# A four-layer graph attention kernel: other step costs for the clock that spaces out row and tile work

## The chip, the core and the metric

The kernel runs on one core of one Trainium2 chip. The metric is the device time of one execution in microseconds (us), the median of the runs shown. Engines are named as in the profile: PE is the matrix engine (TensorE), PEld its loading of weights, DVE the vector engine, ACT the scalar engine, POOL the engine that issues the gathers here (GpSimd), SP the one that issues most plain transfers.

## What is computed

The input is x (4096 nodes by 256 features) and one adjacency matrix adj (4096 by 4096, sparse, denser towards the low node numbers). Four layers of graph attention follow each other, each with a layer norm, a ReLU and a residual. Cut to what matters:

```python
def layer(x, f):                       # the same around all four
    h = relu(layernorm(x))
    return x + f(h)

def f0(h):                             # f1: the same, with elu around it
    g = h @ W.T + b_W
    e = leaky_relu((g @ a1)[:, None] + (g @ a2)[None, :] + b_a, 0.2)
    return softmax(where(adj > 0, e, -big), axis=1) @ g

def f2(h):                             # four heads of 64 columns each
    g = einsum("ni,hio->hno", h, W)
    e = leaky_relu(src[:, :, None] + dst[:, None, :], 0.2)
    return concat_heads(softmax(where(adj > 0, e, -inf)) @ g)

def f3(h):                             # two softmaxes, of e and of -e
    p = softmax(where(adj > 0,  e, -big)) @ h
    q = -softmax(where(adj > 0, -e, -big)) @ h
    return elu(concat(p, q) @ wtrans)
```

## The kernel before, in words

Nodes are cut into 32 tiles of 128 (T = 0 to 31). A target tile's sum over its sources is worked in *steps*. A **dense** unit takes four target tiles at once and goes through all 32 source tiles, one per step (in layer 2 one per step and head). A **listed** unit takes one target tile and goes through the first four source tiles and then through CAPS[T] groups of 128 listed sources, which are gathered by row number from a table in DRAM (L1228, s_gg). How many blocks of four tiles are dense is DENSE = (4, 2, 1, 1) for layers 0 to 3; the rest is listed.

In `run` (L1191) one plan of steps goes through four stages, by LEAD = (0, 2, 3, 6): a step is fetched (its gather is issued), two steps later `begin` (layer 2's share of the weights on ACT, L1018), three steps later `weigh` (the weights on DVE, L1032, L1041), six steps later `multiply` (PE, L1068, in layer 2 L1093). All engines work through their queues in the order in which this plan issues the instructions.

Between the steps other work is strewn in, held in two queues of Python generators, `posts` and `lists_q`:

- what ends a tile: `end1`, `end2`, `end3` (layer 1: ACT and DVE, L1131 to L1135; layer 2: a copy s_o on ACT, L1148, transposes s_oT on PE, L1155, then DVE, L1160 to L1165);
- `node_rows` (L683), which makes the rows of the next layer for two tiles: statistics (L693, L694), Ln and Exp on ACT (L697, L698), z (L702), three small DVE instructions (L709 to L711), transposes s_tp on PE (L716), copies s_hT on ACT (L718), projections s_pj on PE (L748), their scaling on ACT or DVE (L770 to L783) and the store of the rows to the table (L729);
- in layer 0, `list_sources` (L819), which finds the lists of sources from the adjacency matrix, a block of four tiles at a time (DVE L825 to L875, PE idx_ps L900, the list in L910). Once a tile's list exists, its masks are gathered (`gather_masks`, L928), one after each dense step of layer 0; what is then still missing is gathered in one go before that tile's first row gather (L1223).

A generator yields the time for which it wants to be left alone (4.0, 3.0, 1.5, 1.0 or nothing). The delay is measured by a clock that is not the chip's: after each step's multiply the plan adds the step's assumed `cost` to it. Then up to `rates` entries of the queues go on, of the first two in `posts` and the first in `lists_q`, if the clock has passed the time that they wait for. So a delay of d lasts as many steps as their costs take to add up to d. Where a step needs rows which are not made yet, `ensure` (L676) drives the posts on without regard to the clock. After the dense steps with which a layer opens, all rows of the layer must be there before the first gather: layer 1 opens with 16 dense steps, layer 2 with 36, layer 3 with 16 (L1476).

The transposes s_tp, s_sT (L966) and s_oT, the projections s_pj and the lists' idx_ps share a pool of two PSUM buffers (tag "mm", `ps_mm`); the sums of the units share six (`ps_acc`), gathered rows seven or nine in SBUF.

In layer 1 the masks of tiles 8 to 15 come with the gathered rows and are copied away by ACT (L1240); so ACT's queue waits for the gathers there. In layer 2 that holds for tiles 4 to 7.

The cost lines that the change touches are the default of `Unit.__init__` (L985), the listed units of layer 0 (L1378), the dense units of layers 1 and 2 (L1463; layers 0 and 3 take the default) and the listed units of layers 1 to 3 (L1471).

## Time and profile before

| what | us |
|---|---|
| median of 3 runs | 1701.94 (1697.17 to 1703.21) |
| the profiled execution | 1796.08 |
| its span, first to last instruction | 1794.3 |
| layer 0 (in the profiled execution) | about 30 to 517 |
| layer 1 | 517 to 841 |
| layer 2 | 841 to 1366 |
| layer 3 | 1366 to 1783 |

The profiled execution is longer than the runs without a profile, so durations from the trace add up to its own time and not to the median. In the profile's lines, Lnnn is the line of the kernel, `out<-in` names the tiles, x is the number of instructions, and the bracket at the end of a timeline line gives the idle time of the engine before it and what ended it. A matrix multiplication in f32 shows as two records.

### The profile page before, as it was taken

Reading aid. Unit: us, or ns where it says so; the run is one execution under the profiler, and the core shown is the slowest. Engines: PE = TensorE matmul, PEld = TensorE weight load, DVE = VectorE, ACT = ScalarE, POOL = GpSimd, SP = SyncE. Lnnn points to the kernel's source line nnn. Section 1 sums busy time; section 2 is a strip of 40 time slices with the busy share of each in tenths; the row PEclk is TensorE's granted clock in tenths of the full one; section 3 lists DMA queues with packets and bytes.
Section 4 is the critical chain, followed back from the end, with each engine's and each line's share of the span. In section 5 each row is a group of like instructions: output and inputs, shape, how many; then the busy total and the mean of one; then the engine's idle time right before and its main releaser. Section 6 shows DMA issues by size and latency. Waiting matters only on the chain.

```text
span 1794.3 us, 29158 instructions
## 1 busy us (share of the span) xinstructions
PE 1660.2 (93%) x9268; PEld 1384.3 (77%) x9268; DVE 1319.1 (74%) x3908; ACT 631.0 (35%) x1915; POOL 960.5 (54%) x930
## 2 busy tenths in 40 slices
PE   6998899799889999888999999988889999999997
PEld 4886777678778778676577878788888888888876
DVE  6787899777744676556788888877785566777755
ACT  5630010020120232333467666788884011111101
POOL 8836666646535656553353444444561666655453
PEclk9999999999879999989999999999999999999999
DMA  7888778853244444543233332323342665666553
GB/s 258 301 299 281 242 244 251 264 143 110 60 135 138 134 117 134 147 132 106 82 94 86 90 90 81 98 82 83 99 116 75 197 208 175 183 180 178 160 165 107
DMA packets 152237, 274.70 MB, mean 153 GB/s; under 512 B 21423, under 2 KB 75340, under 8 KB 152076
## 3 DMA queue, kind: packets, MB, share of 16 engines
q0 software_dynamic: 45584, 130.39, 26.8%
q1 hardware_dynamic: 105656, 141.83, 24.2%
q8 instruction: 77, 1.26, 0.3%
q14 instruction: 84, 0.69, 0.1%
q10 hardware_dynamic: 836, 0.53, 0.1%
HBM read 231.76 MB, written 40.90 MB: 152 GB/s over the span
## 4 chain that ended last, share of the span: by engine, by line
PE 78%; DVE 8%; issue 4%; DMA 3%; POOL 3%; ACT 2%; another core or an unknown queue 2%; SPq 0%; POOLq 0%; DVEq 0%; ACTq 0%
PE s_acc L1068 44%; PE s_accm L1093 20%; PE s_pj L748 8%; DVE s_p L1032 3%; PE idx_ps L900 2%; PE s_tp L716 2%; PE s_sT L966 2%; DMA s_gg<-table,idx 1%; DMA s_raw<-in_adjT 1%; ACT s_p L1018 1%; DVE s_m L1322 1%; POOL s_z L702 1%; POOL s_gg L1228 1%; DVE s_p L1041 0%
## 5 line engine op out<-in xcount | busy, mean ns | idle before, releaser
L1228 POOL DMA_INDIRECT s_gg<-table,idx x715 | 757.9, 1060 | 733.5 <-PE s_acc L1068 228.6
L1032 DVE SCALAR_TENSOR_TENSOR s_p<-s_grow,s_gg,mlist 128x128 f32<-128x128 f32 x994 | 310.1, 346 | 143.0 <-PE s_acc L1068 85.9
L1068 PE MATMUL s_acc<-s_gg,s_p 128*128 128x257 f32 x1430 | 353.8, 390 | 9.9 <-DVE s_p L1032 7.8
L1068 PEld LDWEIGHTS s_acc<-s_gg,s_p 128*128 128x128 f32 x1430 | 270.5, 194 | 53.6 <-DVE s_p L1032 12.6
L1068 PE MATMUL s_acc<-g,s_p 128*128 128x257 f32 x1152 | 292.5, 397 | 14.2 <-DVE s_p L1032 5.3
L1068 PEld LDWEIGHTS s_acc<-g,s_p 128*128 128x128 f32 x1152 | 220.0, 198 | 49.7 <-issue 12.3
L1032 DVE SCALAR_TENSOR_TENSOR s_p<-s_grow,pre,mpre 128x128 f32<-128x128 f32 (+1 forms) x576 | 189.2, 369 | 49.4 <-PE s_acc L1068 30.5
L1093 PE MATMUL s_accm<-s_p,s_gg 128*65 128x128 f32 x1744 | 204.7, 273 | 1.7 <-issue 1.6
L1068 PE MATMUL s_acc<-s_gs,s_p 128*128 128x257 f32 x896 | 203.6, 380 | 0.0
L1032 DVE SCALAR_TENSOR_TENSOR s_p<-s_grow,s_gs,s_ms 128x512 f32<-128x512 f32 x224 | 161.9, 748 | 50.7 <-PE s_accm L1093 24.7
L748 PE MATMUL s_pj<-s_w,s_hT 128*128 128x259 f32 (+3 forms) x640 | 175.9, 417 | 24.9 <-ACT s_hT L718 9.5
L1093 PEld LDWEIGHTS s_accm<-s_p,s_gg 128*65 128x65 f32 x1744 | 193.2, 138 | 5.3 <-issue 2.8
L1018 ACT ACTIVATE s_p<-s_grow,s_minus,s_gg 128x128 f32<-128x128 f32 x436 | 186.7, 485 | 25.9 <-PE s_accm L1093 15.0
L1068 PE MATMUL s_acc<-pre,s_p 128*128 128x257 f32 x768 | 184.0, 384 | 5.5 <-ACT s_y L1179 3.5
L1068 PEld LDWEIGHTS s_acc<-s_gs,s_p 128*128 128x128 f32 x896 | 169.4, 190 | 24.7 <-issue 0.6
L972 ACT ACTIVATE s_grow<-s_sT 128x256 f32<-128x256 f32 (+2 forms) x136 | 46.8, 367 | 379.3 <-PE s_sT L966 260.9
L748 PEld LDWEIGHTS s_pj<-s_w,s_hT 128*128 128x128 f32 x640 | 126.3, 205 | 56.4 <-ACT s_hT L718 14.2
L1068 PEld LDWEIGHTS s_acc<-pre,s_p 128*128 128x128 f32 x768 | 144.5, 192 | 28.4 <-ACT s_y L1179 3.9
L928 POOL DMA_INDIRECT mlist<-mask_t,idx x105 | 122.1, 1162 | 65.1 <-issue 30.0
L1093 PE MATMUL s_accm<-s_p,pre 128*65 128x128 f32 (+1 forms) x928 | 122.2, 286 | 2.6 <-issue 2.5
L1093 PEld LDWEIGHTS s_accm<-s_p,pre 128*65 128x65 f32 x928 | 105.1, 139 | 21.0 <-issue 18.3
L1018 ACT ACTIVATE s_p<-s_grow,s_minus,pre 128x128 f32<-128x128 f32 x224 | 95.0, 485 | 23.2 <-issue 18.9
(126 smaller groups left out, 1743.5 us busy)
## 6 DMA issues: line engine op xcount, KB each, us to landing
s_raw<-in_adjT SPq DMA_DIRECT2D x128, 512.0 KB
s_gs<-table SPq DMA_DIRECT2D x28, 516.0 KB
s_gg<-table,idx POOLq DMA_INDIRECT x715
mask_t<-s_m SPq DMA_DIRECT2D x35, 256.0 KB
table<-s_g SPq DMA_DIRECT2D x28, 258.0 KB
s_ms<-mask_t SPq DMA_DIRECT2D x28, 256.0 KB
table<-s_m SPq DMA_DIRECT2D x21, 256.0 KB
table<-g SPq DMA_DIRECT2D x8, 516.0 KB
```

The source lines that it names most:

```text
L702: (nc.gpsimd if L.l == 0 else nc.vector).tensor_scalar(z, x[:, T, :], mv[:, k, 0:1], 0.0, op0=ALU.subtract, op1=ALU.max)
L716: nc.tensor.transpose(tp[:, c, :], zs[k][:, c * P : (c + 1) * P], ident)
L748: nc.tensor.matmul(ps, lhsT=hT[:, c, :], rhs=L.w[:, c, k * (D + 6) : k * (D + 6) + cols], start=(c == 0), stop=(c == 1),)
L900: nc.tensor.matmul(ps[:, 0:cap], lhsT=first[:, :, j % half], rhs=val[:, 0:cap, j * IT + t], start=(j == 0), stop=(j == JT - 1),)
L928: nc.gpsimd.indirect_dma_start(out=mlist[:, OFFS[T] + k, :], out_offset=None, in_=mask_t[T // IT], in_offset=bass.IndirectOffsetOnAxis(ap= ...
L966: nc.tensor.transpose(ps[:, h - h0, it, :], L.s[:, T0 + it, h : h + 1].to_broadcast([P, P]), ident)
L972: nc.scalar.activation(grow[:, h1:h2, :], ps[:, h1 - h0 : h2 - h0].rearrange("p h a b -> p h (a b)"), AF.Exp, scale=scale,)
L1018: nc.scalar.activation(w[:, h, :], u.grow[:, h, :], AF.Relu, scale=g[h][:, n - 1 : n], bias=minus)
L1032: nc.vector.scalar_tensor_tensor(p[:, k, :], u.grow[:, h, :], g[k][:, n - 1 : n], m, op0=ALU.min if L.l == 3 and h == 1 else ALU.max, op1= ...
L1068: nc.tensor.matmul(u.accs[it][h], lhsT=p[:, k, it * P : (it + 1) * P], rhs=g[k][:, 0:n], start=first, stop=last,)
L1093: nc.tensor.matmul(u.regions[h], lhsT=g[k][:, 0 : DH + 1], rhs=p[:, k, :],  start=first and (u.nt > 1 or h == 0), stop=last, skip_group_ch ...
L1228: nc.gpsimd.indirect_dma_start(out=wide, out_offset=None, in_=L.table, in_offset=bass.IndirectOffsetOnAxis(ap=index[T][:, k : k + 1], axis=0),
```

## The change

Only costs are exchanged; no instruction is added or taken away.

```diff
-        def __init__(u, L, T0, nt, n, get, big=None, heads=None, like=None, cost=1.7, nact=0, rates=(2, 0, 0), per=1):
+        def __init__(u, L, T0, nt, n, get, big=None, heads=None, like=None, cost=2.1, nact=0, rates=(2, 0, 0), per=1):
...
-            u = Unit(L0, T, 1, DP + CAPS[T], listed_sources(L0, T, gat0), cost=0.45, rates=(1, 2, 0))
+            u = Unit(L0, T, 1, DP + CAPS[T], listed_sources(L0, T, gat0), cost=0.55, rates=(1, 2, 0))
...
-                    cost=0.9 if l == 2 else 1.7,
+                    cost=0.55 if l == 2 else 2.1,
...
-                L, T, 1, DP + CAPS[T], listed_sources(L, T, gat), cost=(0, 0.9, 1.2, 0.9)[l], nact=(0, 0, 2, 0)[l]
+                L, T, 1, DP + CAPS[T], listed_sources(L, T, gat), cost=(0, 0.55, 0.9, 1.05)[l], nact=(0, 0, 2, 0)[l]
```

So a dense step counts 2.1 instead of 1.7 in layers 0, 1 and 3, and 0.55 instead of 0.9 in layer 2 (where a step is one head of one source tile). A listed step counts 0.55 instead of 0.45 in layer 0, 0.55 instead of 0.9 in layer 1, 0.9 instead of 1.2 in layer 2 and 1.05 instead of 0.9 in layer 3.

## The prediction

> **What bounds the kernel now.** I read the page's parts 1 and 2, then stretches cut at the layers' borders, then TensorE's waits in each stretch, then the timeline around the places where rows are spread.

> ```profile
> PE 1660.2 (93%) x9268; PEld 1384.3 (77%) x9268; DVE 1319.1 (74%) x3908; ACT 631.0 (35%) x1915; POOL 960.5 (54%) x930
> ...
> 30.00:517.00 487.00, 445.22 (x2534) 372.59 (x2532) 386.95 (x968) 103.67 (x378) 298.96 (x259) 0.94 0.69 214
> 517.00:841.00 324.00, 290.35 (x1298) 242.07 (x1299) 195.44 (x598) 85.20 (x305) 173.95 (x174) 0.95 0.48 137
> 841.00:1150.00 309.00, 304.22 (x1900) 221.42 (x1899) 270.86 (x794) 196.04 (x527) 132.28 (x121) 0.99 0.31 86
> 1150.00:1352.00 202.00, 180.13 (x1456) 168.95 (x1455) 158.48 (x563) 170.84 (x500) 98.10 (x95) 0.98 0.35 97
> ...
> 1366.00:1783.00 417.00, 411.27 (x1912) 355.39 (x1910) 275.24 (x877) 50.36 (x132) 228.59 (x218) 1.00 0.57 170
> ```

> Part 1, then stretches (length; busy PE, PEld, DVE, ACT, POOL; clock, DMA): layer 0, layer 1, layer 2 with its dense block, layer 2's tiles alone, layer 3. TensorE is busy 1660.2 of 1794.3 us. The 134.1 us of idle lie 41.8 in layer 0, 33.7 in layer 1, 4.8 and 21.9 in layer 2, 5.7 in layer 3, 26.3 before 30 and after 1783. This execution took 1796.08 us, the median is 1701.94: 94 us of it are absent from ordinary runs, and TensorE's busy time would nearly fill them. So less than half of the idle can be real, and no change of order can win much. I apply differences in us to the median unscaled.

> The change moves only work spread by the clock: tile ends, next rows, layer 0's lists. Its places:

> ```profile
> 145.11 0.44 PE L716 MATMUL s_tp<-s_ident,s_z 128*128 128x128 f32 x2 [1.16 <-ACT s_hT L718]
> 146.01 1.14 PE L748 MATMUL s_pj<-s_w,s_hT 128*128 128x259 f32 x4 [0.46 <-ACT s_hT L718]
> ...
> 499.61 1.03 POOL L928 DMA_INDIRECT mlist<-mask_t,idx  x1 [0.31 <-issue]
> 506.51 0.95 POOL L928 DMA_INDIRECT mlist<-mask_t,idx  x1 [0.30 <-issue]
> 507.76 0.94 POOL L1228 DMA_INDIRECT s_gg<-table,idx  x1 [0.30 <-issue]
> ...
> 584.63 1.17 PE L748 MATMUL s_pj<-s_w,s_hT 128*128 128x268 f32 x4 [1.91 <-issue]
> ...
> 867.06 1.97 PE L748 MATMUL s_pj<-s_w,s_hT 128*128 128x268 f32 x8
> 869.71 0.42 DVE L776 TENSOR_TENSOR s_g<-s_pj,s_re 128x256 f32<-128x256 f32 x1 [0.48 <-ACT s_re L774]
> 872.91 0.95 POOL L1228 DMA_INDIRECT s_gg<-table,idx  x1 [42.66 <-PE s_accm L1093]
> 883.09 1.72 PE L1093 MATMUL s_accm<-s_p,s_gg 128*65 128x128 f32 x11
> ...
> 819.30 0.69 PE L716 MATMUL s_tp<-s_ident,s_z 128*128 128x128 f32 x2 [4.70 <-issue]
> ```

> These are timeline lines (start, us, engine, line, work, idle before). They show a transpose held while a list's idx_ps occupies one of two s_mm buffers; a burst of mask gathers ahead of layer 0's last tile; a projection held in layer 1; layer 2's last rows, 4 to 7, projected just before its first gather; a transpose held in layer 1's end, where ACT's copies of masks wait for gathers.

> [...] the transpose at 819.30 held every later matmul of TensorE for 4.70 us. [...] the last row is ready at 869.71 + 0.42 = 870.13 and the gather that reads the table starts 2.8 us later.

> **The change part by part.** A delay d at cost c lasts ceil(d/c) steps. So 1.5 in layer 1's tiles goes from 2 steps to 3 and 4.0 from 5 to 8; in layer 2's dense steps 4.0 goes 5 to 8, 1.5 from 2 to 3; in layer 2's tiles 1.0 goes 1 to 2 and 3.0 from 3 to 4; in layer 0's dense steps a list's 4.0 goes 3 to 2. In layer 3 the row and tile delays of 1.5 stay 1 step (dense) and 2 (tiles). No instruction is added or dropped; each is only placed earlier or later. I counted every placement by pump's rule.

> Real pitch, from groups of matmuls: 16 records of a dense step pair in layer 1 take 614.11 - 610.64 = 3.47 us, so a record 0.217, a dense step (8) 1.74, a tile step (2) 0.43. In layer 2, 20 dense records take 8.75, so a dense step (2) 0.87; a tile step (8) 3.66/4 = about 0.9. The new 0.55 for layer 2's dense steps is thus below the trace.

> *Layer 0's end, a gain.* The first list's index comes 3 steps sooner, and mask gathers, one per dense step, run about 8 steps further ahead. Before, dense steps end with 8 gathers undone: two fall before tile 30's rows (479.74, 480.99), six before tile 31's (499.61 to 507.46). After, five. A gather takes 0.95 plus 0.30: 1.25 us. The two have 6.1 us of POOL idle behind them at 482.4, so they are hidden. The sixth stands straight before the last tile's six row gathers, where TensorE waits: -1.3. Bounds -3.8 (three count) and 0.

> *Layer 0's lists, a loss.* Lists that come 3 to 5 steps sooner meet the next layer's row work at other steps. Transposes placed while an idx_ps is open go from 7 to 13: rows 4 to 11 come in, 14 and 15 go out, 3 pairs net. With one buffer, second transpose and projection queue behind ACT's s_hT: 1.16 + 0.46 here, 0.32 + 0.46 at 131: 1.2 us a pair, 3.6. Dense steps behind have up to 3 weights ready, so part returns later: +2.5. Bounds -2 (the pairs removed at 470 and 482 idled 1.98 and 2.88) and +6. DVE and DMA are otherwise unchanged.

> *Layer 1's tiles, a gain.* One more tile step lies between Ln and transposes and between transposes and projections: 3 matmuls become 4, 0.43 us more cover for s_hT, 11 or 12 times, at most 5. TensorE's waits at L748 in this stretch sum to 4.0 (issue) + 1.2 (s_hT) + 0.9 (s_grow). At 582.7 to 584.2 ACT and TensorE stop together, which no placement explains, so half is not ours. In the last 8 tiles the longer holds (3.76, 4.70) end when a gather has landed; moving a transpose two tile steps later saves 0.87 before it, but its projections move 3 steps later and then wait nearer the tile's end. Together -2; bounds -5 and +2. End1 holds its accumulator 5 steps both before and after (4.0 is passed by two dense steps at 2.1), so psum is no wait.

> *Layer 2's opening, a loss.* Count steps from layer 2's first multiply. Tiles 4 to 7 end layer 1 together and go two at a time. Projections of 14/15, 4/5, 6/7 follow steps 8, 16, 24 before (867.06 is 24 x 0.87 + 4.5 of row work after 841.5) and 11, 21, 31 after. The first gather is fetched in step 35, first multiplied in 41. So the last row's store comes 7 steps x 0.87 = 6.1 us later: the gather starts at 872.9 + 6.1 = 879.0, lands about 2.0 later (731.78 to the copy at 734.00 is 2.2), plus 0.9 of ACT's two weights and 0.7 of DVE and passing on: 882.6 against 883.1 needed. Behind it nine more at 1.29 each against 0.9 per step: the tenth lets its multiply end near 895.3, where it ended at 894.05 with some 0.8 of common stop in it. +1.5; bounds 0 and +4. Queued behind these gathers on POOL are the next tile's, which 6 dense steps cover.

> *Layer 2's tiles, a loss.* s_oT holds a s_mm buffer a step longer, and rows bunch: projections under an open s_oT go from 20 to 28, two pairs of tiles more. Such projections idled 0.95 (1254.30) and 1.59 (1308.14); two pairs have four waits at most, 5. But one more step between copy and s_oT covers holds like 1.04 and 1.70, and ACT, busy 170.8 of 202, is near the bound. +1.5; bounds -3 and +5. Rows for layer 3 are all ready in the same step before and after (about 5 before its first gather), so layer 3 costs nothing.

> Sum: -1.3 + 2.5 - 2 + 1.5 + 1.5 = +2.2: profiled 1796.1 to 1798.3, median 1701.9 to 1704.

> **The rivals.** *Nothing*: waits end with gathers and ACT whatever the placement; 1702. For it: idle is small, all sums above are of a few matmuls. Against: the 6.1 us at the opening are plain placement.

> *Slower*: the opening of layer 2. Three steps (2.6 us) of margin remain between last store and first gather. If gathers land 1 us later than taken, or if a placed instruction slips past step 35 so that ensure forces it, the first ten gathers start from an empty POOL: the chain of Ln, transposes, copies, projections and stores (861 to 873 in the trace, some 12 us) stands before tile 8 with nothing behind it. It decides once the last store falls beyond step 35. With layer 0's and 2's losses at their upper ends: 12 to 14, so 1715.

> *Faster*: in layer 1's last third the holds of 2.72, 2.62, 3.76 and 4.70 (13.8) vanish since the waiting instruction moves behind its releaser, and the three masks count fully: 1702 - 10 = 1692. For it: sums of 2 to 5 us at one instruction. Against: these tiles have 8 to 10 gathers of 1.25 us, 10 to 12.5 us a tile, against 9.8 of TensorE work, so POOL takes over.

> **How the numbers follow.** Forecast 0.42, nothing 0.16, slower 0.28, faster 0.14. The likeliest's own range is 1698 to 1711 (the bounds' sums -14 and +19, mostly cancelling). The range for 8 in 10 takes in part of both outer rivals: 1692 to 1718. A measurement here tells 0.5% (8.5 us) from no change: faster 0.14, same 0.57, slower 0.29.

> **What would show it.** Layer 2's first gather near 879 on the old scale, the last projections there 6 us later; five mask gathers, not six, before layer 0's last tile; more waits of L716 on s_hT between 120 and 400; four tile matmuls between transposes and projections in layer 1; layer 3 as long as before. Wrong would be a layer 3 that changed, forced chains at a border, or layer 1's stretch moving by over 8 us.

## The result and the profile after

After: 1723.28 us (median of 4 runs, 1719.97 to 1726.49); before beside it: 1699.56 (4 runs, 1694.95 to 1703.21). The ratio is 1.0141, 95% interval 1.0106 to 1.0175: 1.4% slower, 24 us, where the forecast ended at 1718.

The trace shown of before (span 1794.3) can't be set against this one: in three sessions, each on another chip, this kernel took 1782 to 1821 us in run after run (medians 1793.93, 1797.86 and 1800.35), in the others 1694 to 1708, and that trace looks like one of the former; the reason wasn't looked for. So the sentence ahead of the prediction that a profiled execution is longer than the runs is wrong: before was traced again (run e1_before_again, span 1695.5 in a run of 1697.28), and all layers below are compared with that trace. First part 1 of the page, then the stretches (length; busy PE, PEld, DVE, ACT, POOL; clock, DMA), cut at the ends of layer 0, layer 1, layer 2's dense block and layer 2. The kernel after:

```profile
PE 1631.9 (95%) x9268; PEld 1374.4 (80%) x9268; DVE 1321.2 (77%) x3908; ACT 635.6 (37%) x1915; POOL 973.6 (56%) x930
...
30.00:491.00 461.00, 434.31 (x2532) 366.02 (x2532) 390.34 (x981) 104.32 (x380) 304.59 (x258) 0.97 0.73 227
491.00:798.00 307.00, 280.32 (x1293) 238.65 (x1294) 190.67 (x586) 82.99 (x297) 176.08 (x174) 0.96 0.50 142
798.00:1108.00 310.00, 302.27 (x1870) 221.58 (x1869) 265.15 (x777) 197.62 (x510) 141.72 (x121) 0.98 0.31 84
1108.00:1306.00 198.00, 191.93 (x1615) 183.60 (x1614) 172.61 (x616) 184.21 (x545) 105.58 (x98) 1.00 0.38 106
1306.00:1714.00 408.00, 408.00 (x1910) 354.86 (x1909) 282.00 (x875) 50.12 (x131) 217.55 (x218) 1.00 0.60 173
```

The same view of e1_before_again:

```profile
PE 1623.1 (96%) x9268; PEld 1369.2 (81%) x9268; DVE 1322.0 (78%) x3908; ACT 633.2 (37%) x1915; POOL 950.6 (56%) x930
...
30.00:485.00 455.00, 432.52 (x2543) 365.31 (x2541) 389.43 (x985) 106.23 (x387) 296.02 (x259) 0.98 0.75 231
485.00:784.00 299.00, 280.11 (x1293) 238.19 (x1292) 192.35 (x585) 82.35 (x295) 171.13 (x174) 0.96 0.51 146
784.00:1093.00 309.00, 309.00 (x1969) 229.38 (x1968) 277.84 (x822) 209.11 (x560) 139.36 (x125) 1.00 0.32 88
1093.00:1276.00 183.00, 177.84 (x1511) 171.18 (x1510) 159.40 (x566) 170.19 (x495) 99.03 (x93) 1.00 0.39 107
```

Read the count of matmuls beside the length. Layer 1 has 1293 in both, in 307 and in 299 us. From layer 2's first multiply, after does 1870 in 310 us and before 1969 in 309, and the clock is 0.98 and not 1.00.

Layers can be told from the trace: layer 0 ends at L948's matmul, layer 2 runs from the first to the last multiply of L1093. For each layer I summed, over windows of 1 us, TensorE's idle time and its clock loss (busy time times one minus the granted clock; a granted clock of 0.50 is called half clock below):

| layer | before (e1): length, idle, clock loss | after | difference |
|---|---|---|---|
| 0 | 484.6, 37.2, 8.9 | 491.4, 42.5, 10.9 | +6.8 = 5.3 idle + 2.0 clock, near enough |
| 1 | 299.0, 18.9, 8.9 | 306.9, 26.3, 9.2 | +7.9 = 7.4 + 0.3 |
| 2 | 492.1, 5.2, 0.0 | 507.2, 13.8, 5.3 | +15.1, of which 8.6 + 5.3 |
| 3 | 419.8, 10.6, 0.0 | 419.3, 9.5, 0.0 | -0.5 |

So the 29.3 us between the two spans are 20 us of waiting and 7.6 us of a slower clock behind waits, in layers 0, 1 and 2. (This trace of after is the longest of its four runs; the medians are 24 us apart.)

### The profile page after: what moved, and what is told of

It reads as the page before. It is cut to its first block, busy times and chain, and to the rows that moved or that the text cites. A ratio compares the mean times of both kernels' runs of the same rounds, so it can differ in the third digit from the quotient of the medians.

```text
span 1724.8 us, 29085 instructions
## 1 busy us (share of the span) xinstructions
PE 1631.9 (95%) x9268; PEld 1374.4 (80%) x9268; DVE 1321.2 (77%) x3908; ACT 635.6 (37%) x1915; POOL 973.6 (56%) x930
## 3 DMA queue, kind: packets, MB, share of 16 engines
q1 hardware_dynamic: 105656, 141.83, 25.5%
## 4 chain that ended last, share of the span: by engine, by line
PE 50%; DMA 2%; DVE 2%; ACT 1%; issue 1%; POOL 0%; POOLq 0%; ACTq 0%; DVEq 0%
PE s_acc L1068 25%; PE s_accm L1093 20%; PE s_pj L748 3%; DMA s_gg<-table,idx 2%; PE s_sT L966 1%; ACT s_p L1018 1%; DVE s_p L1032 1%; PE s_tp L716 1%; PE s_oT L1155 0%; DVE s_p L1041 0%; ACT mlist L1240 0%; POOL s_gg L1228 0%; DVE s_y L1184 0%; DVE s_out L1135 0%; DVE s_er L1134 0%
## 5 line engine op out<-in xcount | busy, mean ns | idle before, releaser
L1228 POOL DMA_INDIRECT s_gg<-table,idx x715 | 761.5, 1065 | 659.7 <-PE s_acc L1068 216.9
L1032 DVE SCALAR_TENSOR_TENSOR s_p<-s_grow,s_gg,mlist 128x128 f32<-128x128 f32 x994 | 318.0, 349 | 116.7 <-PE s_acc L1068 59.5
L1068 PE MATMUL s_acc<-s_gg,s_p 128*128 128x257 f32 x1430 | 350.0, 390 | 30.4 <-DVE s_p L1032 30.3
L1068 PE MATMUL s_acc<-g,s_p 128*128 128x257 f32 x1152 | 287.8, 392 | 8.2 <-DVE s_p L1032 7.0
L1032 DVE SCALAR_TENSOR_TENSOR s_p<-s_grow,pre,mpre 128x128 f32<-128x128 f32 (+1 forms) x576 | 190.0, 371 | 48.5 <-PE s_acc L1068 34.6
L1093 PE MATMUL s_accm<-s_p,s_gg 128*65 128x128 f32 x1744 | 208.9, 275 | 3.1 <-DVE s_p L1032 2.0
L1093 PEld LDWEIGHTS s_accm<-s_p,s_gg 128*65 128x65 f32 x1744 | 195.8, 139 | 7.5 <-DVE s_p L1041 2.4
L1032 DVE SCALAR_TENSOR_TENSOR s_p<-s_grow,s_gs,s_ms 128x512 f32<-128x512 f32 x224 | 161.4, 751 | 44.1 <-PE s_acc L1068 22.2
L748 PE MATMUL s_pj<-s_w,s_hT 128*128 128x259 f32 (+3 forms) x640 | 164.5, 398 | 11.7 <-ACT s_hT L718 7.3
L928 POOL DMA_INDIRECT mlist<-mask_t,idx x105 | 129.3, 1232 | 56.3 <-issue 27.7
L748 PEld LDWEIGHTS s_pj<-s_w,s_hT 128*128 128x128 f32 x640 | 121.7, 197 | 36.3 <-ACT s_hT L718 11.1
L1093 PE MATMUL s_accm<-s_p,pre 128*65 128x128 f32 (+1 forms) x928 | 118.4, 284 | 0.0
L1093 PEld LDWEIGHTS s_accm<-s_p,pre 128*65 128x65 f32 x928 | 103.8, 138 | 17.3 <-issue 14.3
```

The lines of the kernel that those rows point to most:

```text
L748: nc.tensor.matmul(ps, lhsT=hT[:, c, :], rhs=L.w[:, c, k * (D + 6) : k * (D + 6) + cols], start=(c == 0), stop=(c == 1),)
L928: nc.gpsimd.indirect_dma_start(out=mlist[:, OFFS[T] + k, :], out_offset=None, in_=mask_t[T // IT], in_offset=bass.IndirectOffsetOnAxis(ap= ...
L1032: nc.vector.scalar_tensor_tensor(p[:, k, :], u.grow[:, h, :], g[k][:, n - 1 : n], m, op0=ALU.min if L.l == 3 and h == 1 else ALU.max, op1= ...
L1068: nc.tensor.matmul(u.accs[it][h], lhsT=p[:, k, it * P : (it + 1) * P], rhs=g[k][:, 0:n], start=first, stop=last,)
L1093: nc.tensor.matmul(u.regions[h], lhsT=g[k][:, 0 : DH + 1], rhs=p[:, k, :],  start=first and (u.nt > 1 or h == 0), stop=last, skip_group_ch ...
L1228: nc.gpsimd.indirect_dma_start(out=wide, out_offset=None, in_=L.table, in_offset=bass.IndirectOffsetOnAxis(ap=index[T][:, k : k + 1], axis=0),
```

## The experiments

Layers of the traces beside which before takes 1700 us, in us:

| run | layer 0 | layer 1 | layer 2 | layer 3 | ratio to before, 95% interval |
|---|---|---|---|---|---|
| e1 before again | 484.6 | 299.0 | 492.1 | 419.8 | 1.0011 (0.9996 to 1.0026) |
| after | 491.4 | 306.9 | 507.2 | 419.3 | 1.0141 (1.0106 to 1.0175) |
| e2 layer 0 only | 496.7 | 300.2 | 492.3 | 418.8 | 1.0068 (1.0047 to 1.0089) |
| e3 layer 1 only | 483.4 | 307.8 | 492.1 | 419.3 | 1.0036 (1.0024 to 1.0048) |
| e4 layer 2 only | 479.5 | 302.5 | 499.8 | 419.2 | 1.0058 (1.0037 to 1.0078) |
| e5 tile side | 483.6 | 311.5 | 494.2 | 419.3 | 1.0058 (1.0040 to 1.0076) |
| e6 dense side | 503.3 | 299.5 | 500.2 | 418.7 | 1.0148 (1.0123 to 1.0173) |
| e7 other way | 484.7 | 313.4 | 498.9 | 418.7 | 1.0099 (1.0082 to 1.0116) |
| e8 masks off ACT | 486.4 | 292.3 | 493.3 | 419.2 | 0.9949 (0.9929 to 0.9969) |
| e9 the same in after | 497.1 | 292.6 | 501.1 | 418.7 | 1.0060 (1.0041 to 1.0079) |
| e10 later tile in layer 2 | 483.5 | 301.9 | 494.3 | 418.9 | 1.0003 (0.9990 to 1.0017) |
| e15 layer 0 dense only | 497.0 | 302.3 | 495.4 | 418.7 | 1.0076 (1.0052 to 1.0100) |
| e16 the same, lists held back | 484.5 | 299.8 | 492.4 | 419.7 | 1.0007 (0.9993 to 1.0020) |
| e17 filled waits | 484.4 | 300.0 | 494.4 | 420.6 | 0.9985 (0.9974 to 0.9996) |

An unchanged layer varies by some us from trace to trace: layer 0 by 7 (479.5 to 486.4), layer 1 by 3, layer 2 by 3, layer 3 by 2. A row is one trace each, while the ratios rest on all runs; so a difference of 7 us in layer 0, or of 2 in layer 2, proves nothing by itself.

### Which layers: e1 to e4

e1 is the kernel before, unchanged. e2 to e4 make the edits of one layer each:

```diff
-            return Unit(L0, ib * IT, IT, NT, get, big="growb", rates=(2, 2, 1))
+            return Unit(L0, ib * IT, IT, NT, get, big="growb", cost=2.1, rates=(2, 2, 1))
...
-            u = Unit(L0, T, 1, DP + CAPS[T], listed_sources(L0, T, gat0), cost=0.45, rates=(1, 2, 0))
+            u = Unit(L0, T, 1, DP + CAPS[T], listed_sources(L0, T, gat0), cost=0.55, rates=(1, 2, 0))
```

for e2; for e3

```diff
-                    cost=0.9 if l == 2 else 1.7,
+                    cost=0.9 if l == 2 else 2.1,
...
-                L, T, 1, DP + CAPS[T], listed_sources(L, T, gat), cost=(0, 0.9, 1.2, 0.9)[l], nact=(0, 0, 2, 0)[l]
+                L, T, 1, DP + CAPS[T], listed_sources(L, T, gat), cost=(0, 0.55, 1.2, 0.9)[l], nact=(0, 0, 2, 0)[l]
```

and for e4 the same two lines with 0.55 for layer 2's dense steps (1.7 for the others) and (0, 0.9, 0.9, 0.9) for the tiles.

> The kernel before, unchanged, for a second trace. All theories: 1700, ratio 1.00. The first trace took 1796; if 94 us of that belong to the profiling, the new one is near 1790 again, and if they were chance it is near 1700 and the layers' lengths can be set beside those of the changed kernel (layer 0 to 485, layer 1 313, layer 2 508, layer 3 408).

> New costs in layer 0 alone (2.1 and 0.55). Theory A (the loss lies in layer 1's last eight tiles, where DVE's s_r waits behind ACT's copies of masks): 1700, ratio 0.998 to 1.003. Theory B (the loss is the lists of layer 0 falling on other rows): +15 to +24, ratio 1.009 to 1.014. The forecast's own sum for this part is +1.

> New costs in layer 1 alone (dense 2.1, tiles 0.55). Theory A: +12 to +24, ratio 1.007 to 1.014, with waits of 5 to 7 us of s_acc for s_p in the last four pairs of tiles of layer 1. Theory B and theory C (layer 2's opening): ratio 0.998 to 1.002. The forecast's own sum for this part is -2.

> New costs in layer 2 alone (dense 0.55, tiles 0.9). Theory C (late rows at layer 2's opening and rows bunched in its tiles): +10 to +24, ratio 1.006 to 1.014. Theories A and B: ratio 0.998 to 1.003. The forecast's own sum for this part is +3.

Measured: 1700.60, 1710.35, 1706.22 and 1706.72 us. Each layer that was edited is longer by 8 to 12 us, and no other moves beyond the spread above. The three losses (0.68, 0.36, 0.58%) add up to 1.6%, the whole is 1.4%. None of the three theories is the one cause; each has a share. No run changes layer 3's costs alone; in after, which has them too, it takes 419.3 us against 419.8.

### Which side of each layer: e5 and e6

e5 has the tile costs of layers 0 to 2 (0.55, 0.55, 0.9), e6 the dense ones (2.1, 2.1, 0.55).

> Only the tile costs are changed, each in its layer: layer 0's lists 0.55, layer 1's tiles 0.55, layer 2's tiles 0.9; the dense costs stay as before. The layers are read one by one (before: 484.6, 299.0, 492.1, 419.8 us; all edits: 491.4, 306.9, 507.2, 419.3). Theory A, layer 1's end is lost because its tile steps become more numerous between Ln and transposes: layer 1 takes 306 to 308 here. Theory B, layer 0 is lost because a list's 4.0 falls from 3 dense steps to 2: layer 0 stays within 479 to 487 here. Theory C, layer 2 is lost in its opening: layer 2 stays at 492 to 494 here, its first gather starting 31 us after its first multiply, and the clock there stays 1.00. Total under all three: about 1708. The rival to each: the loss comes with the other side, and this run shows 484, 299 and 500.

> The complement of the tile costs: layer 0's dense steps 2.1, layer 1's 2.1, layer 2's 0.55, tile costs as before. Theories A, B and C together: layer 0 takes 490 to 497, layer 1 299 to 302, layer 2 about 500 with its first gather 40.5 us after its first multiply and a stretch at half clock right behind, layer 3 419; total about 1714. Theory A alone falls if layer 1 takes 306 or more here. Theory B falls if layer 0 stays below 487. Theory C falls if layer 2 stays at 492. A fourth theory, that layers disturb each other, would show a sum of this run's and the tile run's losses that is far from the whole's 24 us.

Measured: 1709.06 and 1723.44 us. Layer 1 is lost with the tile cost (311.5 against 299.5), layer 0 with the dense cost (503.3 against 483.6), layer 2 by 8.1 with the dense cost and by 2.1 with the tile cost, which is within the spread. Each theory's place stands. The two losses add up to more than the whole (2.1% against 1.4%), so the sides are not simply additive. e6's layer 0 is also longer than the 490 to 497 us expected: it has 6.7 us more idle than e1's and 14.5 more clock loss.

### The other way: e7

```diff
-                    cost=0.9 if l == 2 else 1.7,
+                    cost=1.4 if l == 2 else 1.7,
...
-                L, T, 1, DP + CAPS[T], listed_sources(L, T, gat), cost=(0, 0.9, 1.2, 0.9)[l], nact=(0, 0, 2, 0)[l]
+                L, T, 1, DP + CAPS[T], listed_sources(L, T, gat), cost=(0, 1.6, 1.6, 0.9)[l], nact=(0, 0, 2, 0)[l]
```

> The costs go the other way: layer 1's tiles 1.6 (a delay of 1.5 is 1 step and not 2, 4.0 is 3 and not 5), layer 2's dense steps 1.4 (4.0 is 3 and not 5), layer 2's tiles 1.6 (3.0 is 2 and not 3); layers 0 and 3 as before. If placing rows and tile ends late is what costs (theories A and C), earlier places cost nothing or gain: layer 2's first gather starts some 28 us after its first multiply, layer 2 takes 488 to 492, layer 1 at most 299, total 1690 to 1700. If the times of before are a local best and any shift collides with something (a rival to both), layers 1 and 2 are each longer by 3 to 8 us and the total is 1705 to 1715. Layer 0 should be 480 to 485 under either.

Measured: 1715.55 us, layer 1 longer by 14.4 and layer 2 by 6.8. The theory that a later place costs and an earlier one gains falls. Layer 1 loses in both directions, so what costs there is hardly the place by itself; the next runs look for what a shift meets.

### Layer 0: e15 and e16, with e11 and e13

e15 has only the dense cost of layer 0. In e16 (and e11, e13: the same kernel) the lists' three delays are stretched so that they last three dense steps again, with all else at 2.1 (one of the three lines):

```diff
-        yield 4.0
+        yield 5.0
```

> Before with layer 0's dense cost 2.1 (which made layer 0 503 us long together with nothing else changed in it) and the lists' three delays of 4.0 stretched to 5.0, so that they last 3 dense steps again and not 2 (5.0 / 2.1 as 4.0 / 1.7); all else on the clock stays at the 2.1. If layer 0 is lost because lists come too early (idx_ps before VectorE's val, transposes under an open idx_ps), layer 0 falls back to 480 to 487 us, the waits of idx_ps on val to about 1.7, total 1696 to 1702. Rival: it is the rows and weights that the 2.1 moves (delays of 1.5 and 15.0): layer 0 stays at 493 or more, total 1708 or more.

> The kernel of e11 again, since there the kernel before itself took 1794 us beside it and no layer can be set against the other traces. Lists come too early: layer 0 is 480 to 487 us (503.3 with the cost of 2.1 and delays of 4.0), total 1696 to 1702. Rival, rows and weights moved by the 2.1: layer 0 is 493 or more, total 1708 or more.

> Before with layer 0's dense cost of 2.1 alone, on the same chip as the next run, so that the two are compared there. Layer 0 is 15 to 20 us longer than that of the kernel before on the same chip, as it was beside the other dense costs (503.3 against 484.6); ratio 1.008 to 1.012. Rival: on this chip the loss is not there (ratio within 0.3% of 1), and then nothing is learnt from e11 and e13 on the lists.

> As e11, beside the run with the 2.1 alone. If the lists' earlier places cost it, the ratio is 0.998 to 1.003 here while the run with the 2.1 alone is over 1.007. If rows and weights cost it, both have the same ratio within 0.2%.

Beside e11 and e13 before took 1793.93 and 1797.86 us: 1.0012 (0.9984 to 1.0041) and 0.9994 (0.9969 to 1.0019), so no loss there either, but no layers to compare. e15 and e16 ran on one chip: 1713.61 and 1699.52 us, ratios 1.0076 and 1.0007. The lists' earlier places cost it, not rows or weights. TensorE's waits in layer 0 of e15 (what waited and for what: us in total, times, longest):

```profile
PE idx_ps L900 <- DVE val L869: 4.5, 2, 2.8
PE idx_ps L900 <- DVE idx L910: 1.5, 1, 1.5
PE idx_ps L900 <- DVE first L875: 1.4, 2, 1.1
PE s_tp L716 <- ACT s_hT L718: 1.4, 3, 0.5
```

and of e16:

```profile
PE idx_ps L900 <- DVE val L869: 1.9, 1, 1.9
...
PE idx_ps L900 <- DVE idx L910: 0.2, 1, 0.2
```

The largest of them in the timeline of e15 (start, us, engine, work, idle before):

```profile
338.51 1.09 DVE L875 TENSOR_TENSOR first<-place,lof 128x1792 f16<-128x1792 f16 x1
...
339.52 0.85 DVE L865 TENSOR_TENSOR val<-lists,hib 128x1344 f16<-128x1344 f16 x1
340.29 0.75 DVE L1032 SCALAR_TENSOR_TENSOR s_p<-s_grow,g,mpre 128x512 f32<-128x512 f32 x1
340.95 0.85 DVE L869 TENSOR_TENSOR val<-val,code 128x1344 f16<-128x1344 f16 x1
341.72 0.28 DVE L1119 COPY den<-s_acc 128x1 f32<-128x1 f32 x3
341.86 0.59 PE L900 MATMUL idx_ps<-val,first 128*128 128x10 f16 x7 [2.76 <-DVE val L869]
```

VectorE has 2.8 us of list work (1.09 + 0.85 + 0.85) with weights between; with one dense step less of delay the matmul L900 stands at the head of TensorE's queue before val is made, and every multiply behind it waits, 2.76 us here. Then the clock, in windows of 4 us of e15:

```profile
336.00:340.00 4.00, 2.00 (x8) 1.44 (x8) 4.00 (x14) 0.00 (x0) 3.39 (x3) 1.00 0.90 251
340.00:344.00 4.00, 2.14 (x18) 1.78 (x19) 4.00 (x16) 0.00 (x0) 1.76 (x3) 0.72 0.70 230
344.00:348.00 4.00, 4.00 (x11) 3.17 (x11) 4.00 (x10) 0.78 (x3) 3.39 (x3) 0.50 0.14 40
```

After the wait TensorE is busy throughout and its clock is 0.50. Against e16, layer 0 of e15 has 6.7 us more idle (44.8 - 38.1) and 6.3 more clock loss (13.9 - 7.6), together 13.0 us where the two lengths differ by 12.5: half of the price is the clock in this pair. e6 has the same edit in layer 0, and its trace is 6.3 us longer there with 0.9 us less idle (43.9): its clock loss is 23.4. So one edit's price in clock differs by 9.5 us between two traces; the last section shows where over half of that arose.

### Layer 1: e8 and e9

In the last eight tiles, ACT's copies of masks (L1240) wait for gathers. e8 is before, e9 is after, both with these 69 copies made by POOL instead, each three gathers later:

```diff
+    waiting = []
...
-                    nc.scalar.copy(kept, m)
+                    if L.l == 2:
+                        nc.scalar.copy(kept, m)
+                        return heads, [g[:, h * L.part : (h + 1) * L.part] for h in heads], m
+                    waiting.append((kept, m))
+                    last = T == 15 and k == CAPS[T] - 1
+                    while len(waiting) > (0 if last else 3):
+                        nc.gpsimd.tensor_copy(*waiting.pop(0))
```

> Before, with layer 1's mask copies (L1240, 69 of them, in its last eight tiles) made by GpSimd, each three gathers after its own, so that ScalarE makes none of them there. Theory: ScalarE's Ln and Exp stand behind copies that wait for gathers, VectorE's s_r (L709) waits 6.0 us for the Exp and holds the weights behind it, and so TensorE idles 4.9 us at each of the last pairs, with half a clock for some 5 us after each. Then those four waits vanish or fall below 2 us, s_r's wait falls from 6.0 to below 2, layer 1 falls from 299 to 280 to 290 us, total 1682 to 1692. Rival: GpSimd's gathers (1.25 us each) pace these tiles whatever ScalarE does, and the copies on GpSimd come on top: layer 1 stays at 297 to 305, the waits end with gathers, total 1698 to 1706.

> The kernel after, with the same move of layer 1's mask copies to GpSimd. If the tile cost of 0.55 hurts only by what stands behind the Exp on VectorE, layer 1's loss of 8 us over before vanishes with the wait: layer 1 is within 3 us of that of before with the same move (280 to 290), total 1700 to 1710. If gathers pace these tiles, layer 1 keeps its 8 us over it: 305 or more, total 1720 to 1730. Layers 0 and 2 as in the kernel after (491 to 497, 500 to 507).

What this takes away, in the timeline of after:

```profile
712.04 0.35 DVE L702 TENSOR_SCALAR s_z<-x,s_mv 128x256 f32<-128x256 f32 x1
...
716.18 0.30 ACT L1240 COPY mlist<-s_gg 128x128 uint8<-128x128 uint8 x1 [1.54 <-DMA s_gg<-table,idx]
...
717.98 0.30 ACT L1240 COPY mlist<-s_gg 128x128 uint8<-128x128 uint8 x1 [1.30 <-DMA s_gg<-table,idx]
718.18 0.20 ACT L698 ACTIVATE s_r<-s_r 128x2 f32<-128x2 f32 x1
...
718.41 0.16 DVE L709 SCALAR_TENSOR_TENSOR s_r<-s_mv,s_r 128x2 f32<-128x2 f32 x1 [6.01 <-ACT s_r L698]
...
719.04 1.66 DVE L1032 SCALAR_TENSOR_TENSOR s_p<-s_grow,s_gg 128x128 f32<-128x128 f32 x6
719.10 1.22 PE L1068 MATMUL s_acc<-s_gg,s_p 128*128 128x257 f32 x2 [6.89 <-DVE s_p L1032]
```

It reads upwards: TensorE waits 6.89 us for weights; VectorE made none because L709 stood ahead of them in its queue, 6.01 us, for ACT's Exp (L698); the Exp stood behind copies that wait for gathers. The trace of before has the same knot (there L709 waits 6.02 us at 706.29), but its transposes stand ahead of the wait. TensorE's waits in layer 1 of e1_before_again:

```profile
PE s_sT L966 <- ACT s_hT L718: 7.7, 2, 4.9
PE s_tp L716 <- DVE s_r L711: 4.9, 1, 4.9
PE s_tp L716 <- DVE s_r L709: 4.8, 1, 4.8
```

of after:

```profile
PE s_acc L1068 <- DVE s_p L1032: 25.0, 10, 6.9
```

and of e9:

```profile
PE s_acc L1068 <- DVE s_p L1032: 12.0, 13, 1.6
```

VectorE's wait for the Exp in layer 1 of after and of e9 (17.4 us in e1, 1.4 in e8):

```profile
DVE s_r L709 <- ACT s_r L698: 21.1, 9, 6.0
...
DVE s_r L709 <- ACT s_r L698: 1.3, 6, 0.2
```

Measured: e8 1692.70 us, layer 1 292.3; e9 1710.36 us, layer 1 292.6. The long waits are gone in both and so is the difference of 8 us between the two costs: what stood behind the copies on ACT, by the traces the Exp, is the cause of layer 1's loss. The size of the gain was expected at 9 to 19 us and is 7: with the knot gone VectorE waits for gathers themselves (21 waits, 28.4 us in the end of layer 1 of e9), which POOL now issues at one per 1.5 us, with a copy of 0.3 between. The kernel e8 is faster than before and after.

### Layer 2: e10

e4's kernel, with the first listed tile 6 dense steps later:

```diff
-        alone, over_tiles = ((0, 0), (16, 24), (36, 14), (16, 28))[l]
+        alone, over_tiles = ((0, 0), (16, 24), (42, 14), (16, 28))[l]
```

> Layer 2's two costs alone as before (dense 0.55, tiles 0.9, which made layer 2 499.8 us long), and the first listed tile put 6 dense steps later (42 dense steps ahead of it and not 36; the same dense steps are then spread thinner over the next 14 tiles). If the opening's loss is only that the last rows are late for the first gathers, the gathers then land before they are wanted: no wait of TensorE in the first 120 us, clock 1.00 there, layer 2 at 492 to 494, total 1698 to 1701. Rival: the gathers are only moved and the tiles behind, with fewer dense steps between them, wait for them instead: layer 2 stays at 498 or more.

The first gather in e1_before_again, 31.4 us after the first multiply at 783.6:

```profile
814.96 0.94 POOL L1228 DMA_INDIRECT s_gg<-table,idx  x1 [42.52 <-PE s_accm L1093]
```

in after, 40.5 us after the first multiply at 798.3, and who waited for it:

```profile
838.75 0.94 POOL L1228 DMA_INDIRECT s_gg<-table,idx  x1 [52.70 <-PE s_accm L1093]
...
842.00 0.46 PEld L1093 LDWEIGHTS s_accm<-s_p,s_gg 128*65 128x65 f32 x4 [2.20 <-DVE s_p L1032]
842.01 0.70 PE L1093 MATMUL s_accm<-s_p,s_gg 128*65 128x128 f32 x4 [1.96 <-DVE s_p L1032]
```

and TensorE's waits in layer 2's first 120 us, after:

```profile
PE s_pj L748 <- ACT s_hT L718: 4.8, 1, 4.8
PE s_accm L1093 <- DVE s_p L1032: 2.0, 1, 2.0
PE s_accm L1093 <- DVE s_p L1041: 0.9, 2, 0.7
```

e10:

```profile
PE s_accm L1093 <- DVE s_p L1032: 0.8, 1, 0.8
PE s_accm L1093 <- DVE s_p L1041: 0.6, 1, 0.6
```

Measured: 1700.09 us, layer 2 494.3 (499.8 in e4). In e10 1.4 us of waiting are left, the clock stays 1.00, and the loss is gone but for 2 us, no more than the spread (e5, with the tile cost alone, has 2.1). So the opening's loss is that the last rows are late for the first gathers. They are late for two reasons. By the plan, the last projections stand 7 steps later: they start 32.0 us after the first multiply in after, 25.5 in e1. And the row, once made, takes longer to be stored: from its end on VectorE to the first gather it is 5.4 us in after and 5.4 to 5.5 in e4, e6, e9 and e10, against 2.8 in e1 and 2.7 to 2.8 in e2, e3, e5 and e7. In the five long ones a load of 516 KB (s_gs, L1433) was issued 0.6 us ahead of the last store (L729) on SP's queue, which the shift had brought together; no run takes that load away, so this part is read from the traces alone. The wait of 4.8 us in after is another one: a copy s_hT stands on ACT behind weights that wait for gathers, four of which took 4.53, 4.98, 2.49 and 2.07 us on POOL from 871 to 886 where the seven behind them take 0.94 to 1.06. In e4, e6 and e9, with the same dense cost, this wait isn't there, and layer 2 is only 8 to 9 us longer than before; so some 6 of the 15 us in the trace of after are not the change's usual price. Why it comes in this one trace is open.

### The clock behind a wait: e12, e14 and e17

The clock in after behind that wait of 4.8 us (windows of 1 us; the last three columns are clock, DMA, GB/s):

```profile
887.00:888.00 1.00, 1.00 (x10) 0.79 (x8) 0.88 (x5) 0.04 (x1) 0.76 (x1) 1.00 0.53 135
888.00:889.00 1.00, 0.03 (x1) 0.00 (x0) 0.60 (x2) 0.62 (x2) 0.94 (x1) 1.00 0.45 89
890.00:891.00 1.00, 0.00 (x0) 0.00 (x0) 0.61 (x2) 0.38 (x1) 0.69 (x2) 0.74 0.57 93
893.00:894.00 1.00, 1.00 (x3) 0.80 (x4) 0.51 (x2) 0.46 (x2) 0.92 (x1) 0.50 0.50 118
895.00:896.00 1.00, 1.00 (x3) 0.77 (x3) 0.91 (x2) 0.96 (x4) 0.40 (x1) 0.50 0.21 80
897.00:898.00 1.00, 1.00 (x10) 1.00 (x9) 0.00 (x0) 0.23 (x2) 0.00 (x0) 0.85 0.00 0
```

TensorE stops at 888.0, the clock falls to 0.50 some 2.5 us later, stays there for 4 us after work has begun again at 892.9, and rises to 1.00. Before and after it, 10 matmuls go through in a microsecond, in between 3 to 5 (some of these are wider).

To test whether the price comes of the length, three waits at layer 1's end in before were filled with idle transposes, just ahead of them:

```diff
-            for c in range(2):
+            for c in list(range(2)) * (12 if L.l == 2 and T in (8, 10, 12) else 1):
```

> Before, with the first transposes of three row pairs (tiles 8, 10 and 12, at the end of layer 1) made 12 times over: 66 idle transposes of some 0.14 us more, which stand just ahead of three waits of 4.9, 4.8 and 4.9 us. Nothing else changes its place. If a long stop of TensorE costs its own length and the clock behind it as well, the filled waits are some 2 us long, the half-clock stretches behind them (7, 6 and 7 us before) go, and the kernel becomes shorter though it does more: layer 1 falls from 299 by 5 to 9 us, total 1690 to 1695. Rival: the half clock has another cause, or a 2 us wait brings it as well: layer 1 stays at 297 to 303 and the total at 1698 to 1702.

> The kernel of e12 again, for the same reason. If a long stop costs the clock behind it as well: the three waits are some 2 us long, no half clock behind them, layer 1 falls from 299 by 5 to 9 us, total 1690 to 1695. Rival, a 2 us wait brings the half clock too or it has another cause: layer 1 stays at 297 to 303, total 1698 to 1702.

> As e12. Only if the kernel before takes about 1700 us here can layer 1 be set against the first traces: then 5 to 9 us less in layer 1 (clock behind the waits 1.00) if the length of the wait brings the half clock, 297 to 303 if not. On a chip where the kernel before takes 1790 or more, no difference beyond 0.3%, as in e12 and e14.

Beside e12 and e14 before took 1793.93 and 1797.86 us: ratios 1.0026 (1.0001 to 1.0050) and 1.0016 (0.9994 to 1.0038). Beside e17 it took 1699.68: 1698.10, ratio 0.9985 (0.9974 to 0.9996). The second and third of the filled waits in e17:

```profile
731.53 2.78 PE L716 MATMUL s_tp<-s_ident,s_z 128*128 128x128 f32 x24
736.90 0.44 PE L716 MATMUL s_tp<-s_ident,s_z 128*128 128x128 f32 x2 [2.59 <-ACT s_grow L972]
...
758.24 2.78 PE L716 MATMUL s_tp<-s_ident,s_z 128*128 128x128 f32 x24
763.54 0.44 PE L716 MATMUL s_tp<-s_ident,s_z 128*128 128x128 f32 x2 [2.52 <-ACT s_grow L972]
```

The waits became 3.5, 2.6 and 2.5 us (4.9, 4.8, 4.9 in e1), the half-clock stretches 7, 3 and 0 us (7, 7, 7). So shorter waits bring less half clock, but layer 1 is as long as before (300.0), not 5 to 9 us shorter as expected. Some 7 us of idle transposes cost nothing. What a faster clock gains, the run hardly tests: over the whole of layer 1 half clock fell only from 23.9 to 17.9 us, since a stop of 2.6 us at 676 brought 3.4 us of it here and the same stop (2.7 us) none in e1, and the clock loss fell by 0.8 us (9.0 to 8.2). The brackets say that here the end of a wait is set by ACT. That the half clock costs time only where TensorE is the bound, as in layers 0 and 2, fits this but isn't shown.

### All three together: e18

The kernel after with the edits of e16, e9 and e10.

> The kernel after, all its costs kept, with each of the three causes taken away by its own edit: the lists' delays 5.0 in place of 4.0, layer 1's mask copies on GpSimd three gathers later, layer 2's first listed tile 6 dense steps later. If these three are the whole loss, the layers are 481 to 487, 290 to 294, 492 to 496 and 419 us, the total 1685 to 1697, ratio to before 0.993 to 0.998. If there is a fourth cause or they disturb each other, the total is 1700 or more.

Before took 1800.35 us beside it: 1800.30, ratio 1.0008 (0.9986 to 1.0031), where 0.993 to 0.998 was expected. Against the first trace of before (span 1794.3), layer 1 is 7 us shorter (312.5 against 319.6) and layer 2 is 14 us longer (537.8 against 524.0; e11 to e14, which leave it as it was, have 519 to 523), with 8 stretches of half clock against 3, most of them among its tiles alone. So there is no loss against before, but the gain of the moved copies is used up by something in layer 2: the three causes disturb each other there, or a fourth remains. After itself was not run beside such a time of before, so which it is stays open. What is shown is each cause in its own layer.

## Why the prediction was wrong

Its likeliest number, 1704, was 19 us too low. Three terms of its sum failed: layer 1's tiles had the wrong sign (-2 for +7.9), layer 0's lists (+2.5) and layer 2's opening (+1.5) were several times too small (12.5 and 5.5), because waits of other engines and the half clock behind a stop were put at nothing. By its steps:

- **"So less than half of the idle can be real, and no change of order can win much."** Wrong. I put the 94 us between the trace and the median down to profiling. e1's idle, in an execution as long as the ordinary runs, is 72.4 us (1695.5 - 1623.1), more than half of the 134.1. The change added 20 us to it, and e8 took 7 us off the kernel.
- **"I counted every placement by pump's rule."** It holds for what the plan issues, and for POOL, whose order is written by hand. It doesn't hold for the order in which PE, ACT and DVE take their work, which differs from the plan's: in both kernels L709 follows z (L702) directly on VectorE, where the plan puts at least two steps of weights between them, and the Exp stands behind copies of masks for which gathers come 6 us later. The sentence ahead of the prediction that all engines work in the plan's order is wrong for these three.
- **Layer 0's end, -1.3.** The placement came true: five mask gathers (472.10 to 477.09), not six, stand before the last tile's rows. The gain didn't: the wait for that tile is 4.37 us at 482.22, and in e1 it is about the same in sum (4.5), in several pieces.
- **Layer 0's lists, +2.5.** What I counted is there: five transposes behind s_hT at 0.46 each, 2.3 us, none in e1. What I didn't count made the loss: idx_ps behind val (+2.6 in e15 against e16) and behind the list's other VectorE work, and a half clock behind these. e15 against e16 is 12.5 us. I wrote that VectorE was "otherwise unchanged"; its work was, but the delay that covered it was what the change cut.
- **Layer 1's tiles, -2 (bounds -5 and +2).** Wrong in sign: +7.9. I moved a transpose and a projection against TensorE's queue and left alone the instruction that others wait for, L709 on VectorE. I had seen that ACT's copies wait for gathers there, but not what stood behind them on ACT.
- **Layer 2's opening, +1.5 (bounds 0 and +4).** The mechanism was right and the term too small. The first gather came 9.1 us later (40.5 - 31.4), not 6.1: the 7 steps came true (6.5 us), but the 2.8 us from the last row to the gather, read at one place of one trace, were taken as fixed and became 5.4. Putting the first tile later takes back 5.5 us (499.8 in e4, 494.3 in e10). e4's opening has 3.6 us of waits (2.5 on L1032 and 1.1 on L1041), e10's 1.4, and e4 has 1.5 of half clock behind them, which I had not priced.
- **Layer 2's tiles, +1.5.** The size is not contradicted: +2.1 in e5, +2.2 in e10, both within the spread. Its mechanism wasn't looked at.
- **Layer 3, 0.** Right: -0.5 in after.
- **The bounds.** The upper ones add up to +17, not +19, and the eight gathers from 872.91 to 883.52 follow each other by 1.33 us, not 1.29. Neither changes the forecast.

The rival "slower" named the opening of layer 2 and gave 1715: a true part of the loss, but 5.5 us of it. The rival "faster" said that the long holds of layer 1 would vanish when the waiting instruction moved behind its releaser. They do vanish when the releaser is freed (e8), by 7 us; shifting the waiting instruction lengthened them in both directions (e5, e7).

What no step priced is the clock: each wait was charged its length alone. In the traces the clock falls to 0.50 behind a stop, for 3.41 us at the shortest, and stops of 1.5 to 2 us were followed by it in 9 of 42 cases, see the last section.

## What to carry over

When delays are counted in steps, ask for each delay what work of another engine it covers, and read from the trace when that work ends, before asking what the moved instruction does to its own queue. Follow a long wait to the instruction that holds the queue, engine by engine, and then move what that one waits for; moving the waiter only moved the wait here (layer 1 took 311.5 us in e5 and 313.4 in e7, against 292.3 with the copies moved in e8). And charge a stop of TensorE of over 2 us (88 of the 103 counted below were followed by half clock) with some 2 us of clock loss as well, where TensorE is the bound. The 2 us are an estimate from the wait at 888 in after, half of the 4 us in work at 0.50; that a stop costs less elsewhere isn't shown.
